# Where a one-core, four-layer kernel lays the zeros of its padded tensor, and which engine builds the first channels' taps

## The chip, the cores and the metric

The kernel runs on one core of a Trainium2 chip. The metric is device time in microseconds of one execution, as the median of several runs. The engines are named as in the profile: PE is TensorE's matmul and PEld its weight loads, DVE is VectorE, ACT is ScalarE, POOL is GpSimd and SP is SyncE, which here only issues DMA transfers. "Granted clock" is the share of full speed that TensorE was given.

## The reference

An image tensor `x` of 32 images, 192 channels and 56 x 56 pixels passes through four layers, each of the form `x = x + layer(groupnorm(x))`, with 32 groups of 6 channels. Cut to what matters:

```python
# layer 0: agent attention (6 heads, 49 agents) with a 3x3 depthwise convolution of v, then a projection
# layer 1: a two-way WKV scan over the 3136 pixels, sigmoid gate, layer norm, projection
# layer 2: each four channels are shifted by a rounded offset and smoothed with their own 3x3 Gaussian
x = x + _L0_conv_ref(_gn(x), ...)
x = x + _L1_conv_ref(_gn(x), ...)
x = x + _L2_conv_ref(_gn(x), L2_conv_offset)
# layer 3: convolution with a 55x55 implicit filter by FFT
x = x + _L3_conv_ref(_gn(x), ...)

def _L2_conv_ref(inp, offset):
    R = jnp.round(offset)                       # one (x, y) shift for each 4 channels
    x_src = jnp.arange(Wn)[None, :] - Ri[:, 0:1]
    x_ok = (x_src >= 0) & (x_src < Wn)          # zero where the shifted pixel lies outside
    ...
    kern = jnp.exp(-sq / (2.0 * SIGMA ** 2)); kern = kern / kern.sum(axis=(1, 2), keepdims=True)
    return conv_general_dilated(out, kern, ..., feature_group_count=Cn)
```

## The kernel before

The kernel has four stages in one program, one after the other; all data are float32.

1. `make_filter` builds the spectra of layer 3's filter (to about 164 us).
2. `attention` does layer 0, image by image: 32 turns of one loop. Two image tiles alternate: at the start of a turn the next image is loaded (`ready.image`, L392 and L394), and at its end the finished image is stored to the DRAM tensor `x1` (L863, L865), behind its sums `st_a` and `st_c` (L860, L862).
3. `scan_pairs` does layer 1 on pairs of images. It begins with loads of its weights (L936, L941, L942) and of attention's sums (L1063, L1065), prepares weights on PE (L955, L961), and then streams `x1` (L1018). Its result goes to the DRAM tensor `x2`.
4. `channel_blocks` does layers 2 and 3 channel by channel, in groups of six, for all 32 images at once.

`x2` is laid out for stage 4: for each channel 2 x 57 rows of 16 x 112 numbers, of which 56 hold an image row and the other 56 are a gap that must be zero, so that a row read at a shifted address runs into zeros. Attention writes these zeros: a small SBUF tile `zeros` (L460 sets it) is the source, and each channel's gaps are one DMA from SP (L869, 399 KB in 1824 pieces of 224 bytes). There are 192 of them, six at the end of each of the 32 image turns, right behind that image's stores. A dependency of the kind "NoSync" keeps them behind the store on SP's queue: it fixes the order of issue and waits for nothing.

Inside an image turn, `seen` is called twice: once for `gq` (when the first of four column blocks has been weighed) and once for the next image's `gk` (late in the turn); a further call stands ahead of the loop. Each copies a 65-row result into `once` and sends it to the constant tile `gq_c` or `gk_c` with one DMA on SP (L566, 597 KB), where it is repeated eight times. In the loop's second half, `moments` reads the next image (L485 and on).

In stage 4, `prepare(c)` is called four channels ahead of use. It loads a channel's shifted rows into one of three `shifted` tiles (L1618), multiplies them by the norm's scale on POOL (L1619), and applies the three horizontal taps: ACT makes the first (L1622) and, for each of the other two, a product in `more` (L1625), which POOL adds (L1626). `matrix(n)` builds, once for four channels, a 114 x 114 matrix that does the vertical shift and taps: three tap matrices (L1567), two additions (L1571, L1572), all on POOL, then one matmul (L1574) and a copy (L1576). `shift` loads the unshifted rows (L1635), multiplies by the matrix on PE (L1641) and adds (L1642); `middle` and `centre` take the group's mean off (L1661), and `analyse` and `synthesise` do the spectral convolution of the group before (L1683 to L1732). A tile with the tag `spare` has three buffers, which `more` and `sq` of `centre` share.

The order of instructions on each engine is not written out by hand: the framework orders them when the program is built, so that work that is ready earlier can stand ahead of its place in the text. Each engine then runs its own queue in that order.

The functions that the change touches, and what calls them, with the line numbers of the profile:

Of the kernel before, what the change touches and what calls it, by code (L numbers as in the profile page):

```python
# [23 lines left out]
ALU = mybir.AluOpType  # L24
# [4 lines left out]
C = 192  # L29
T = 96  # L30
S = 56
# [13 lines left out]
HA = HEADS * AG  # L45
GROUP = C // 32
# [361 lines left out]
def attention(ctx: ExitStack, tc: tile.TileContext, a, ready, x1, st_a, st_c, x2, gaps):  # L408
# [9 lines left out]
    nc = tc.nc  # L418
    NB = x1.shape[0]
# [9 lines left out]
    def psum():  # L429
        return pp.tile([128, 2, BANK], F32, name="ps", tag="ps")  # L430
# [4 lines left out]
    n = C + 1  # L435
# [9 lines left out]
    NK = len(WIDTHS)  # L445
# [12 lines left out]
    zeros = cp.tile([2 * (S + 1), LEAD], F32, name="zeros", tag="zeros")  # L458
    for t in (*agents_b[0], *agents_b[1], v_a, v_c, zeros):
        nc.gpsimd.memset(t, 0.0)  # L460
    for at in (0, x2.shape[0] - LEAD):
        nc.sync.dma_start(out=x2[at : at + LEAD].unsqueeze(0), in_=zeros[0:1])

    def small(name, shape):
        return sp.tile(shape, F32, name=name, tag=name)

# [88 lines left out]
    def seen(ag, w, to_c, name):  # L555

        ps = psum()
        for i, cols in enumerate((slice(0, 128), slice(128, C + 1))):
            n = (128, 65)[i]
            mm(ps[:n, i, : 4 * AG], w[0][:, cols], ag[0], start=True, stop=True)  # L560
            mm(ps[:n, i, 4 * AG : HA], w[1][:, cols], ag[1], start=True, stop=True)
        g = small(name, [128, HA])
        nc.scalar.copy(g, ps[:, 0, :HA])
        c = sp.tile([65, HA], F32, name="once", tag="once", bufs=1)
        nc.scalar.copy(c, ps[0:65, 1, :HA])
        nc.sync.dma_start(out=to_c[0:65], in_=c.unsqueeze(1).to_broadcast([65, 2 * NK, HA]))  # L566
        return g

    def normed(x, rs, nb, j):
# [72 lines left out]
    def turn_v(j, v):  # L642

        _, _, ns = sizes(j)
        vT = wp.tile([SUB, 4, 3 * 128], F32, name="vT", tag="vT")
        for s0 in range(0, ns, 2):
            ps = psum()
            for i in range(2):
                px = slice((s0 + i) * SUB, (s0 + i + 1) * SUB)
                for c in range(3):  # L650
                    nc.tensor.transpose(ps[:SUB, i, c * 128 : (c + 1) * 128], v[:, c, px], ident)
            nc.scalar.copy(vT[:, s0 : s0 + 2], ps[:SUB, :, : 3 * 128])
        return vT
# [152 lines left out]
    for b in range(NB):  # L806
        x, more = nxt, b + 1 < NB
        if more:
            nxt = ready.image(nc, a, b + 1)
        low, sums = small("low", [PAIR, NK, 3]), small("sums", [PAIR, NK, 3])  # L810
        got = sp.tile([PAIR, NK, C], F32, name="got", tag="got", bufs=1)
        turned, asked, back = {}, {}, {}
        for j in range(NK):
            prs = weigh(j, gk, low, sums)
            if j == 0:
                gq = seen(ag, wqT, gq_c, "gq_a")
            vT = turn_v(j, v[j])
            if j > 0:
                halves = gather(j - 1, *turned[j - 1])
            if j + 2 < NK:  # L820
                v[j + 2] = find_v(j + 2)
            turned[j] = turn(j, prs), vT
            if j > 0:
                settle(j - 1, halves, got)
            if j + 1 < NK:
                o[j + 1] = convolve(j + 1)
            elif more:
                mv, pools = moments(nxt)
        halves = gather(NK - 1, *turned[NK - 1])
        asked[0] = ask(0, gq)  # L830
        settle(NK - 1, halves, got)
        values = join(low, sums, got)
        done, o = o, {}
        st = small("st", [128, 2, 9])
        for t in range(1, NK + 2):
            if t < NK:
                asked[t] = ask(t, gq)
            if more and t == 1:
                mean, d = spread_of(mv)
            if more and t == 2:  # L840
                rs, nb = scaling(mean, d, pools)
                normed(nxt, rs, nb, 0)
            if t <= NK:
                back[t - 1] = turn_back(t - 1, asked[t - 1])
            if more and t in (3, 4):
                v[t - 3] = find_v(t - 3)
            if t >= 2:
                project(t - 2, done[t - 2], x, st)
            if t <= NK:
                answer(t - 1, back[t - 1], values, done[t - 1])  # L850
            if more and t == 2:
                ag = find_agents(b + 1, pools)
                normed(nxt, rs, nb, 1)
            if more and t == 3:
                gk = seen(ag, wkT, gk_c, "gk_a")
                normed(nxt, rs, nb, 2)
            if more and t == 4:
                o[0] = convolve(0)
                normed(nxt, rs, nb, 3)
        nc.sync.dma_start(out=st_a[:, b % 2, b // 2], in_=st[:, 0])  # L860
        for h, r in HALVES:
            nc.sync.dma_start(out=st_c[b % 2, :, h, b // 2], in_=st[r, 1])  # L862
        nc.sync.dma_start(out=x1[b, 0:128], in_=x[0].rearrange("p y x -> p (y x)"))  # L863
        for h, r in HALVES:
            stored = nc.sync.dma_start(  # L865
                out=x1[b, 128:C, 1568 * h : 1568 * h + 1568], in_=x[1][r].rearrange("p y x -> p (y x)")
            )
        for c in range(C * b // NB, C * (b + 1) // NB):
            laid = nc.sync.dma_start(  # L869
                out=gaps[c].rearrange("s h g w -> (s h) g w"),  # L870
                in_=zeros[:, 0:S].unsqueeze(1).to_broadcast([2 * (S + 1), NB // 2, S]),
            )
            behind = mybir.DependencyInfo(mybir.DependencyClass.NoSync, mybir.DependencyReason.DATA)
            tc.add_manual_dep(laid.ins, stored.ins.name, behind, reason="no burst")


class _Pairs:
# [640 lines left out]
def channel_blocks(ctx: ExitStack, tc: tile.TileContext, shifts, k, flat_x2, x2, rs2, spectra, out):  # L1518
# [8 lines left out]
    nc = tc.nc  # L1527
    NB = out.shape[0]
# [15 lines left out]
    for rows, shape in CHANNEL:  # L1544
        n = int(np.prod(shape))
        t = fixed[:rows, at : at + n]
# [15 lines left out]
    def matrix(n):  # L1562

        if n not in made:
            t = [wp.tile([PR, PR], F32, name=f"tap{f}", tag=f"tap{f}", bufs=1) for f in range(3)]
            for f in range(3):
                nc.gpsimd.tensor_scalar(  # L1567
                    t[f], diff_y, found[:, n, 6 + f : 7 + f], found[:, n, 3 + f : 4 + f], ALU.is_equal, ALU.mult
                )
            mat = wp.tile([PR, PR], F32, name="mat", tag="mat", bufs=3)  # L1570
            nc.gpsimd.tensor_tensor(t[0], t[0], t[1], ALU.add)  # L1571
            nc.gpsimd.tensor_tensor(mat, t[0], t[2], ALU.add)  # L1572
            ps = psum()
            nc.tensor.matmul(ps[:PR, :PR], lags, mat, start=True, stop=True)  # L1574
            rows = wp.tile([PR, PR], F32, name="rows", tag="rows", bufs=3)
            nc.vector.tensor_copy(rows, ps[:PR, :PR])  # L1576
            made.clear()
            made[n] = rows
        return made[n]

    def psum():
        return pp.tile([128, BANK], F32, name="ps", tag="ps", bufs=4)
# [16 lines left out]
    def prepare(c):  # L1599

        if c >= C:
            return
        n, j = divmod(c, GROUP)
        if j == 0:
            scales[n] = sp.tile([PR, GROUP, NI], F32, name="scale", tag="scale", bufs=3)
            for s in range(2):
                nc.sync.dma_start(
                    out=scales[n][(S + 1) * s : (S + 1) * (s + 1)],
                    in_=rs2[c : c + GROUP, s].partition_broadcast(S + 1),
                )  # L1610
        i = c // 4
        if c % 4 == 0:
            begin_at[i] = nc.values_load(
                begins[0:1, i : i + 1], engines=(mybir.EngineType.SP,), min_val=LEAD - S, max_val=LEAD + S
            )
        t = shifted[c % len(shifted)]
        there = flat_x2[bass.ds(begin_at[i] + c * SPAN, SPAN)].rearrange("(p g w) -> p g w", p=PR, w=PITCH)
        nc.sync.dma_start(out=t[:, :, 1 : S + 1], in_=there[:, :, 0:S])  # L1618
        nc.gpsimd.tensor_tensor(t, t, _bc(scales[n][:, j], [PR, NI, S + 2]), ALU.mult)  # L1619
        y = wp.tile([PR, NI, S], F32, name="smooth", tag="smooth", bufs=5)  # L1620
        taps = [found[:, i, f : f + 1] for f in range(3)]
        nc.scalar.activation(y, t[:, :, 0:S], AF.Copy, scale=taps[0])  # L1622
        for f in (1, 2):
            more = wp.tile([PR, NI, S], F32, name="more", tag="spare", bufs=3)
            nc.scalar.activation(more, t[:, :, f : f + S], AF.Copy, scale=taps[f])  # L1625
            nc.gpsimd.tensor_tensor(y, y, more, ALU.add)  # L1626
        smooth[c] = y
        rows_of[c] = matrix(i)
# [301 lines left out]
```

## Time and profile before

| What | Value |
|---|---|
| Median of 3 runs | 12221.74 us |
| Lowest, highest | 12216.5, 12241.55 us |
| The profiled execution's own time | 12216.98 us |
| Its span, first to last instruction | 12215.1 us |
| Mean granted clock of TensorE | 0.958 |
| Busy: PE, PEld, DVE, ACT, POOL | 90%, 54%, 88%, 59%, 28% |
| Instructions: DVE, ACT, POOL | 14722, 14690, 2568 |
| First and last zero transfer (L869) issued | 354.2 us, 4952.6 us |
| Stores of the last image issued | 4922.7 to 4928.2 us |
| First POOL instruction of the channel stage | 8444.3 us |

The span is cut by stage into about 0 to 164 us (filter), to 4923 us (attention), to 8444 us (scan) and to the end (channels). In rows of the timeline the first number is the start in us from the span's start, the second how long the row's instructions took from first to last, then the engine, the line, the operation, the tiles written and read, and how many. A name such as `SPq` or `DVEq` is an engine's queue. A bracket at the end of a row gives idle time ahead of it and what ended that. In rows of the waits, an engine and line are followed by what they waited for, the sum in us, how often, and the longest. Rows of the windows give the busy time of PE, PEld, DVE, ACT and POOL, with the number of instructions in brackets, then the granted clock, the mean share of time that the 16 DMA engines were busy, and what they moved.

### The profile page before, as it was taken

Reading aid. Unit: us, or ns where it says so; the run is one execution under the profiler, and the core shown is the slowest. Engines: PE = TensorE matmul, PEld = TensorE weight load, DVE = VectorE, ACT = ScalarE, POOL = GpSimd, SP = SyncE. Lnnn points to the kernel's source line nnn. Section 1 sums busy time; section 2 is a strip of 40 time slices with the busy share of each in tenths; the row PEclk is TensorE's granted clock in tenths of the full one; section 3 lists DMA queues with packets and bytes.
Section 4 is the critical chain, followed back from the end, with each engine's and each line's share of the span. In section 5 each row is a group of like instructions: output and inputs, shape, how many; then the busy total and the mean of one; then the engine's idle time right before and its main releaser. Section 6 shows DMA issues by size and latency. Waiting matters only on the chain. (4 is left out here: it accounts for less than half of the span.)

```text
span 12215.1 us, 157485 instructions
## 1 busy us (share of the span) xinstructions
PE 11030.6 (90%) x57358; PEld 6623.6 (54%) x57358; DVE 10753.1 (88%) x14722; ACT 7146.9 (59%) x14690; POOL 3400.5 (28%) x2568
## 2 busy tenths in 40 slices
PE   6999999999999999688888888886999999999999
PEld 3555555555555555333333333333666666666666
DVE  6888888888888888799999999996888899898897
ACT  3555555555555555466666666665666666666665
POOL 0000000000000000455555555555343343343330
PEclk9999999999999999899999999997999999999999
DMA  2222222222222222243334334334333333333331
GB/s 70 57 57 57 59 58 64 59 59 59 63 61 57 57 57 49 73 103 96 97 101 104 93 97 104 98 96 100 71 68 64 67 70 64 67 70 64 67 69 32
DMA packets 1959211, 876.56 MB, mean 72 GB/s; under 512 B 1821153, under 2 KB 1858292, under 8 KB 1949292
## 3 DMA queue, kind: packets, MB, share of 16 engines
q1 hardware_dynamic: 1948188, 840.69, 30.1%
q10 hardware_dynamic: 10240, 25.70, 0.8%
q8 instruction: 458, 7.50, 0.3%
q14 instruction: 325, 2.66, 0.1%
HBM read 482.13 MB, written 319.29 MB: 66 GB/s over the span
## 5 line engine op out<-in xcount | busy, mean ns | idle before, releaser
L619 DVE SCALAR_TENSOR_TENSOR o<-v_a,att_w,o 128x896 f32<-128x896 f32 (+1 forms) x1024 | 1056.8, 1032 | 467.3 <-ACT v_a L593 337.3
L1142 POOL MEMSET f<- 128x1 f32 x96 | 8.9, 99 | 4769.6 <-DMA st_c<-st 4764.6
L1793 ACT COPY y<-ps 64x252 f32<-64x252 f32 (+1 forms) x2376 | 808.7, 340 | 797.3 <-PE ps L1787 767.6
L1626 POOL TENSOR_TENSOR smooth<-smooth,more 114x896 f32<-114x896 f32 x384 | 866.3, 2259 | 1200.7 <-ACT more L1625 1141.2
L1709 PE MATMUL ps<-fixed,real 84*84 84x112 f32 x6144 | 1093.6, 260 | 0.0
L1709 PE MATMUL ps<-fixed,imag 84*84 84x112 f32 x6144 | 1091.1, 259 | 0.0
L1717 ACT ACTIVATE z<-ps,rs 84x112 f32<-84x112 f32 x3072 | 816.7, 355 | 322.1 <-PE ps L1709 319.5
L1709 PEld LDWEIGHTS ps<-fixed,real 84*84 84x84 f32 x6144 | 790.2, 154 | 158.4 <-issue 129.4
L1135 ACT ACTIVATE q<-q 128x784 f32<-128x784 f32 x384 | 328.5, 855 | 812.4 <-DVE q L1130 641.2
L1709 PEld LDWEIGHTS ps<-fixed,imag 84*84 84x84 f32 x6144 | 765.8, 153 | 0.0
L890 PE MATMUL ps<-sq,fixed 128*128 128x392 f32 x512 | 298.9, 746 | 425.9 <-ACT sq L1213 425.9
L636 ACT ACTIVATE pr<-ps,low 98x896 f32<-98x896 f32 (+1 forms) x384 | 352.3, 918 | 559.9 <-DVE low L634 559.9
L724 PE MATMUL ps<-gq_a,xs_a 128*112 128x294 f32 x1792 | 619.1, 427 | 45.7 <-DVE pq L729 45.7
L1787 PE MATMUL ps<-fixed,padded 114*128 114x168 f32 x3072 | 527.6, 322 | 134.6 <-DVE x L1729 118.3
L619 DVE SCALAR_TENSOR_TENSOR o<-v_c,att_w,o 128x448 f32<-128x448 f32 (+1 forms) x1024 | 638.3, 623 | 6.0 <-ACT v_c L604 0.9
L632 PE MATMUL ps<-xs_a,gk_a 128*98 128x448 f32 (+1 forms) x1536 | 637.1, 495 | 0.0
L633 PE MATMUL ps<-xs_c,gk_c 125*98 125x448 f32 (+1 forms) x1536 | 631.6, 492 | 0.0
L1728 PE MATMUL ps<-z,fixed 84*114 84x448 f32 x1536 | 609.7, 539 | 0.4 <-ACT z L1717 0.4
L725 PE MATMUL ps<-gq_c,xs_c 125*112 125x294 f32 x1792 | 608.3, 421 | 0.0
L890 PE MATMUL ps<-x,weights 128*128 128x392 f32 x1536 | 574.0, 517 | 31.1 <-DVE bv L1164 14.2
L737 ACT ACTIVATE pq<-pq 112x1176 f32<-112x1176 f32 x224 | 265.4, 1185 | 553.0 <-DVE pq L729 430.1
L1787 PEld LDWEIGHTS ps<-fixed,padded 114*128 114x128 f32 x3072 | 473.6, 198 | 206.1 <-DVE x L1729 140.5
(372 smaller groups left out, 29249.8 us busy)
## 6 DMA issues: line engine op xcount, KB each, us to landing
x<-x SPq DMA_DIRECT2D x576, 392.0 KB
x<-x SPq DMA_DIRECT2D x512, 196.0 KB
x<-zeros SPq DMA_DIRECT2D x192, 399.0 KB
shifted<-x SPq DMA_DIRECT2D x192, 399.0 KB
x<-x SPq DMA_DIRECT2D x192, 399.0 KB
out_x<-x SPq DMA_DIRECT2D x384, 196.0 KB
x<-in_x SPq DMA_DIRECT2D x32, 1568.0 KB
x<-x SPq DMA_DIRECT2D x32, 1568.0 KB
```

Of the source, the lines that this page charges most:

```text
L619: nc.vector.scalar_tensor_tensor(dst, tap(i), dww[:, t, i : i + 1], dst, ALU.mult, ALU.add)
L632: mm(ps[P2, h, :n], g[:, cols], xs_a[j][:, px], start=True, stop=False)
L633: mm(ps[P2, h, :n], gk_c[0:KC, 2 * j + h, cols], xs_c[j][0:KC, px], start=False, stop=True)
L724: mm(ps[:SUB, i, :HA], xs_a[j][:, px], g, start=True, stop=False)
L725: mm(ps[:SUB, i, :HA], xs_c[j][0:KC, px], gq_c[0:KC, 2 * j + (q + i) // ns], start=False, stop=True)
L890: mm(out, aa, srcs[t][h], start=True, stop=False)
L1626: nc.gpsimd.tensor_tensor(y, y, more, ALU.add)
L1709: nc.tensor.matmul(ps[:84, i * 2 * S : (i + 1) * 2 * S], part[:, i0 + i].rearrange("p s u -> p (s u)"), f3[:, m, :], start=(m == 0), stop= ...
L1717: nc.scalar.activation(z[:, i0 + i].rearrange("p m w -> p (m w)"), ps[:84, i * 2 * S : (i + 1) * 2 * S], AF.Copy, scale=q.rs[:, i0 + i : i ...
L1728: nc.tensor.matmul(got, f4[:, m, :], z[:, i0 : i0 + n, m, :], start=(m == 0), stop=(m == 1))
L1787: nc.tensor.matmul(ps[:, g * 168 : (g + 1) * 168], flat[:, (g0 + g) * 128 : (g0 + g + 1) * 128], f1, start=True, stop=True)
L1793: nc.scalar.copy(y[64 * m : 64 * m + 64, 2 * g0 + i : 2 * (g0 + n) : 2], got[64 * i : 64 * i + 64, :, :, m, :])
```

## The change

The 192 zero transfers are taken off one list, `bare`, in order. A new helper `lay(behind, n)` issues the next `n` of them, each kept behind the instruction `behind` on SP's queue in the same way as before (`issue_after` adds edges of issue order only). Two are laid behind each transfer of `gq_c` or `gk_c`, and four behind the last store of each image but the last, which lays whatever is left. When the list is empty, `lay` issues nothing.

In the channel stage, `matrix(n)` uses DVE for its five elementwise operations where `n` is 0 or 1 (channels 0 to 7), and POOL for all others as before. For channels 0, 2 and 4 the second and third tap are each one SCALAR_TENSOR_TENSOR on DVE (multiply by the tap, add to `y`) in place of ACT's product and POOL's addition. Channels 1, 3 and 5, and all from 6 on, stay as they were.

```diff
+    bare = list(range(C))
+
+    def lay(behind, n):
+
+        with tc.issue_after(behind.ins):
+            for c in bare[:n]:
+                nc.sync.dma_start(
+                    out=gaps[c].rearrange("s h g w -> (s h) g w"),
+                    in_=zeros[:, 0:S].unsqueeze(1).to_broadcast([2 * (S + 1), NB // 2, S]),
+                )
+        del bare[:n]
...
-        nc.sync.dma_start(out=to_c[0:65], in_=c.unsqueeze(1).to_broadcast([65, 2 * NK, HA]))
+        lay(nc.sync.dma_start(out=to_c[0:65], in_=c.unsqueeze(1).to_broadcast([65, 2 * NK, HA])), 2)
         return g
...
-        for c in range(C * b // NB, C * (b + 1) // NB):
-            laid = nc.sync.dma_start(
-                out=gaps[c].rearrange("s h g w -> (s h) g w"),
-                in_=zeros[:, 0:S].unsqueeze(1).to_broadcast([2 * (S + 1), NB // 2, S]),
-            )
-            behind = mybir.DependencyInfo(mybir.DependencyClass.NoSync, mybir.DependencyReason.DATA)
-            tc.add_manual_dep(laid.ins, stored.ins.name, behind, reason="no burst")
+        lay(stored, 4 if more else len(bare))
...
         if n not in made:
+            engine = nc.vector if n < 2 else nc.gpsimd
             t = [wp.tile([PR, PR], F32, name=f"tap{f}", tag=f"tap{f}", bufs=1) for f in range(3)]
             for f in range(3):
-                nc.gpsimd.tensor_scalar(
+                engine.tensor_scalar(
                     t[f], diff_y, found[:, n, 6 + f : 7 + f], found[:, n, 3 + f : 4 + f], ALU.is_equal, ALU.mult
                 )
...
-            nc.gpsimd.tensor_tensor(t[0], t[0], t[1], ALU.add)
-            nc.gpsimd.tensor_tensor(mat, t[0], t[2], ALU.add)
+            engine.tensor_tensor(t[0], t[0], t[1], ALU.add)
+            engine.tensor_tensor(mat, t[0], t[2], ALU.add)
...
         for f in (1, 2):
+            if c < GROUP and c % 2 == 0:
+                nc.vector.scalar_tensor_tensor(y, t[:, :, f : f + S], taps[f], y, ALU.mult, ALU.add)
+                continue
             more = wp.tile([PR, NI, S], F32, name="more", tag="spare", bufs=3)
```

## The prediction

> **What bounds the kernel now.** I read the page's slices first: PE is busy 90% of the span and DVE 88%, each near full for most of it, so the change can only matter where both stand still. Two such places show: a dent near slice 16 (attention gives way to the scan) and the start of the channel stage near 8445 us. I then read the windows, SP's queue and the waits at both, and one image of attention to see whether the zeros cost anything where they now lie.
>
> Stage border, columns: busy time of PE, PEld, DVE, ACT, POOL, then granted clock, DMA share, GB/s:
> ```profile
> 4930.00:4940.00 10.00, 0.00 (x0) 0.00 (x0) 0.00 (x0) 0.00 (x0) 0.00 (x0) 0.50 0.56 103
> 4940.00:4950.00 10.00, 0.00 (x0) 0.00 (x0) 0.00 (x0) 0.00 (x0) 0.00 (x0) 0.50 0.49 71
> 4950.00:4960.00 10.00, 0.00 (x0) 0.00 (x0) 0.00 (x0) 0.00 (x0) 0.00 (x0) 0.50 0.51 71
> ```
> No engine works for 30 us while the DMA engines move 71 GB/s. SP's queue over the same time (start, duration, what it issued), and PE's wait:
> ```profile
> 4926.92 1.23 SPq L865 DMA_DIRECT2D x<-x  x2
> 4928.19 30.03 SPq L869 DMA_DIRECT2D x<-zeros  x6
> 4958.33 5.58 SPq L936 DMA_DIRECT2D passing<-in_scan_o  x1
> ...
> 4965.85 1.83 SPq L1065 DMA_DIRECT2D seen<-st_c  x2
> ```
> ```profile
> PE ps L955 <- DMA x<-zeros: 44.3, 1, 44.3
> ```
> The last image's six zero transfers stand between its stores and the scan's first loads. PE waits 44.3 us in one piece.
>
> One image in the middle of attention, SP again:
> ```profile
> 2257.94 0.90 SPq L566 DMA_DIRECT2D gk_c<-once  x1
> 2274.72 0.33 SPq L863 DMA_DIRECT2D x<-x  x1
> ...
> 2279.95 30.77 SPq L869 DMA_DIRECT2D x<-zeros  x6
> 2310.76 5.77 SPq L392 DMA_DIRECT2D x<-in_x  x1
> 2316.58 1.18 SPq L394 DMA_DIRECT2D x<-in_x  x2
> 2317.87 0.94 SPq L566 DMA_DIRECT2D gq_c<-once  x1
> ```
> Here the same zeros hide: no engine's wait in 2280 to 2427 names a DMA, and PE idles under 10 us of that period. They are close to showing, though: the next image is first read by DVE (L485) at 2329.8, and the transfers end at about 2330.
>
> Start of the channel stage, POOL; the bracket is idle time and its releaser:
> ```profile
> 8469.65 4.23 POOL L1626 TENSOR_TENSOR smooth<-smooth,more 114x896 f32<-114x896 f32 x2
> 8505.77 4.22 POOL L1626 TENSOR_TENSOR smooth<-smooth,more 114x896 f32<-114x896 f32 x2 [2.09 <-ACT more L1625]
> 8515.77 0.43 POOL L1572 TENSOR_TENSOR mat<-tap,tap 114x114 f32<-114x114 f32 x1 [5.78 <-PE ps L1574]
> ```
> and DMA there:
> ```profile
> 8500.00:8510.00 10.00, 3.33 (x4) 1.09 (x4) 2.33 (x3) 2.91 (x3) 7.83 (x4) 0.67 0.42 89
> 8510.00:8520.00 10.00, 6.21 (x18) 4.11 (x18) 4.83 (x7) 0.00 (x0) 4.12 (x5) 0.50 0.18 37
> 8520.00:8530.00 10.00, 1.77 (x6) 1.34 (x6) 5.87 (x6) 5.63 (x6) 9.92 (x5) 0.50 0.21 46
> ```
> From 8450 to 8510 POOL is busy 53.6 of 60 us (sum of the six windows), DVE about 12. The chain of waits runs over POOL's L1567, L1619 and L1626 up to 8583, and over PE and DVE after it. The channel rows load at 0.46 DMA share and about 103 GB/s until 8508, then the DMA engines half idle for 18 us because SP waits (15.2 us at L1618) for a `shifted` buffer that the late POOL has not let go.
>
> **Part 1, zeros taken from the border.** The list of 192 channels shrinks by 2 ahead of the image loop and by 8 in each image (2 behind `gq_c`, 2 behind `gk_c`, 4 behind the stores). 2 + 23 x 8 = 186, so the 24th image lays the last 6, and images 25 to 32 lay none. At the border SP comes to L936 at about 4928.2 instead of 4958.3 (30.1 us), and without back-pressure its 5.58 us become about 0.4 like its neighbours, so the x loads of L1018 start at about 4932.2 instead of 4967.7: 35.5 us. In bytes: 6 x 399 KB = 2.45 MB at 71 GB/s is 34.5 us of queue. Against that: the last stores (2.35 MB at the 202 GB/s of 4920 to 4930) need 11.6 us from 4922.7, to 4934.3. If the scan's loads must wait until those land (a tile laid over theirs), they begin some 2 us later, at 4936, where their data began to flow at about 4966 before: 29, or 28 with one more such step. Nothing else is late next: all five engines are idle, and the scan runs on from there with DVE at 93%. Between 28 and 35.5 I take 33, nearer the byte count, since PE's L955 started within 1 us of the zeros' end. The granted clock is 0.50 there in either case, as PE still idles over 10 us.
>
> **Part 1, zeros inside attention.** Two zeros behind `gk_c`: 0.98 + 5.96 us of SP ((30.77 - 0.98) / 5 = 5.96 each), so SP is free at 2266 and the transfers (11.5 us, behind 3 to 5 for `gk_c`) end at 2273 to 2275; the next issue is at 2274.7. This hole covers them; were it gone, the stores would slip 1 to 2 us, for which only the image load waits, behind four more zeros. Four behind the stores are 0.98 + 3 x 5.96 = 18.9 us instead of 30.8, so the image and then `gq_c` are issued 11.9 us sooner: more slack. Two behind `gq_c`: SP's next issue is 80 us away. Cost 0. As a bound: images take 147.5 or 149.1 us (12 of 30 the long sort), with PE's clock at 0.97 in 2340 to 2400; another mix of these gives between -19 and +29, of which I allow -16 to +12, since attention starts in the same phase.
>
> **Part 2, taps and matrices.** Off POOL come two matrices (3 x 0.75 + 2 x 0.43 = 3.1 us each) and six L1626 (2.1 each): 6.2 + 12.6 = 18.8 of its 53.6. Off ACT come six L1625 (1.04 each). DVE gets ten small operations and six SCALAR_TENSOR_TENSOR; the nearest row is L619 on 128x896, 1.15 us, so 6.9 us into a DVE that is 80% idle there. For an even channel, 4.2 us of POOL become 2.3 us of DVE.
> How much reaches the path: the sixth channel's POOL work now ends at 8510. Loads set a floor: its x leaves SP at 8494.3 and lands near 8497, so at most about 14. POOL walked through (first `shifted` at 8458 as now; 1.74 a channel; 4.2 for each odd one; matrices 2 to 4 in the gaps; channel 5's `shifted` not before 8489, then 1.7 of POOL, one tap of ACT and 4.2) ends at 8497 to 8498: 12 less. What follows (mean, centring, channels 6 on, whose ACT tiles wait for POOL) hangs on that point, and the 18 us hole in the loads lets it move forward.
> Against it stands a row: L1661, a DVE operation with two SBUF inputs, takes 1.07 us at its least and 2.63 beside POOL; POOL's L1619 goes from 1.74 to 2.59, a tap from 0.75 to 3.42. If each of the six new ones met one POOL operation it would wait up to 2.1, and POOL would lose about 1 at each: near 6 less gain. In the worst case, a DVE wait in each chain and POOL still held by taps, the gain is -2. From -2 to 14 I take 11, nearer the walk, as DVE's pairs fall mostly into POOL's waits for loads.
> The Trainium skill (SBUF — State Buffer, Who interferes with whom) says that a DVE instruction with two SBUF inputs and a GpSimd one that reads SBUF exclude each other for a whole instruction; L1661's 2.63 us fits. By that rule alone every one of the six would block once and this part would bring 5; the sum would be 38.
>
> **Sum.** 33 + 0 + 11 = 44 us off the profiled execution's own 12216.98 (span 12215.1): 12173. The median of the three runs, 12221.74, lies 4.8 above that execution; I add 2: 12175. A measurement of this kernel tells 0.2%, or 24 us, from no change.
>
> **Rivals.**
> *Border only, 12186.* POOL keeps its present order: between channel 0's and channel 1's `shifted` it did 8.1 us of matrices 2 to 4, and if the DVE pairs also meet the locks, part 2 gives 0: 12219 - 33. For it: the order on POOL is not the program's, and L1661's spread. Against: 18.8 us leave the busiest engine. Chance 0.12.
> *Start only, 12208.* The zeros hid another wait at the border (stores landing, a tile laid over an older one) or SP issues the zeros late after all: `issue_after` fixes only what they stand behind. 12219 - 11. Against: stores end by 4934 by their bytes, and zeros are ready at once. Chance 0.08.
> *Slower, 12247.* SP takes `gq_c` and its two zeros ahead of the next image's load. Then six zeros precede the load as now, plus `gq_c`'s 3 us, and L485, which now reads within 1 us of landing, starts 3 us late in 24 images: +72, net 12175 + 72. It decides from 44 / 24 = 1.8 us an image. For it: `once` is ready at 2284.7, before SP is free. Against: today it was ready just as early and SP still took the image first. Chance 0.10, all slower outcomes included.
>
> **How the numbers follow.** Forecast 0.70, border only 0.12, start only 0.08, slower 0.10. Both first cases are over 24 us faster: faster 0.82; start only is within: 0.08; slower 0.10. Range: low 12219 - 35.5 - 14 - 16 = 12153; high 12219 - 28 + 2 + 12 = 12205, which leaves out the slower case and parts of the tails. The first two cases alone span 12153 to 12195.
>
> **What would show it.** Right: no zeros after about three quarters of attention; PE's wait at L955 falls from 44.3 to 8 to 16 us; image periods stay at 147.5 and 149.1; channel 5's last L1626 ends 10 to 14 us sooner after the stage's start than its 59.6 now; the 18 us hole in the loads shrinks. Wrong: a wait of PE or DVE for a DMA inside an image; L936 issued later than 4940; DVE's new operations at over 2 us; a channel period over the 114 to 115 us per six channels that the chain shows.

## The result: 0.6% slower, and the profile after

The changed kernel took 12308.13 us (median of 6 runs, 12298.35 to 12315.04) against 12227.83 us of the kernel before beside it (6 runs, 12216.5 to 12241.55): a ratio of 1.0064, interval 1.0051 to 1.0077. The forecast was 12175 us with a range of 12153 to 12205, so the time moved the wrong way and lies outside the range.

Cut at the same three places, the profiled executions show where the time went (us; attention to the last `st_a` store, then border and scan to the stage's first POOL instruction, then the channel stage to the end of the span):

| | attention | border and scan | channel stage | span |
|---|---|---|---|---|
| before | 4923.9 | 3520.5 | 3770.8 | 12215.1 |
| after | 5068.0 | 3490.4 | 3749.0 | 12307.5 |
| difference | +144.2 | -30.0 | -21.7 | +92.4 |

Border and start gained, as forecast, though the last column also holds differences of later groups that do not come from the change (see e3). Attention, which was to cost nothing, lost 144 us. (The change moved the lines: L485 is now L497, L619 is L631, the zeros of L869 are L470, L566 is L578, L872 and L874 are the stores of the sums, L936 is L942, L1567 to L1626 are L1574 to L1636.)

**Attention.** The waits of the whole kernel, DVE, hold one row that the kernel before has not at all:
```profile
DVE st_a L497 <- DMA x<-in_x: 167.8, 23, 8.6
```
DVE waits for the next image's load in 23 images, 7.3 us each. One of them, SP's queue first:
```profile
812.96 0.32 SPq L872 DMA_DIRECT2D st_a<-st  x1
...
817.34 18.68 SPq L470 DMA_DIRECT2D x<-zeros  x4
836.07 5.93 SPq L392 DMA_DIRECT2D x<-in_x  x1
...
843.50 0.93 SPq L578 DMA_DIRECT2D gq_c<-once  x1
844.49 15.21 SPq L470 DMA_DIRECT2D x<-zeros  x2
```
and DVE at that time:
```profile
842.65 0.68 DVE L631 SCALAR_TENSOR_TENSOR o<-v_c,att_w,o 128x448 f32<-128x448 f32 x1
850.58 1.68 DVE L497 BATCH_NORM_STATS2 st_a<-x 128x6 f32<-128x448 f32 x3 [7.25 <-DMA x<-in_x]
852.17 1.13 DVE L631 SCALAR_TENSOR_TENSOR o<-v_a,att_w,o 128x896 f32<-128x896 f32 x1
```
SP behaves as forecast: four zeros, the load, then `gq_c`. What the forecast did not have is the second view. Three of the seven statistics L497 stand between two rows of the convolution L631, where DVE arrives at 843.3, that is 30.4 us after the `st_a` store of that turn. In the kernel before DVE came to the first statistic 54.3 us after that store and did all seven there, as the image that the prediction shows has it:
```profile
2275.57 0.32 SPq L860 DMA_DIRECT2D st_a<-st  x1
...
2329.85 1.16 DVE L485 BATCH_NORM_STATS2 st_a<-x 128x6 f32<-128x448 f32 x2
```
The load is now issued 23.1 us after the store instead of 35.3, and DVE can read it at 850.6, 37.6 us after the store: 12 us of gain for the load, but 7.3 us too late for a read that was moved ahead by 24. PE's and ACT's orders in attention are those of before in the traces; on DVE only these three statistics and one small addition of `got` have changed places in each image.

The other engines, in windows of 10 us (busy PE, PEld, DVE, ACT, POOL, granted clock, DMA share, GB/s), and PE's wait for the weights that ACT makes from DVE's result:
```profile
840.00:850.00 10.00, 9.98 (x100) 7.52 (x99) 3.32 (x5) 8.47 (x20) 0.00 (x0) 1.00 0.90 240
850.00:860.00 10.00, 7.49 (x24) 3.25 (x22) 9.42 (x13) 0.00 (x0) 0.00 (x0) 0.99 0.66 124
860.00:870.00 10.00, 5.88 (x56) 5.24 (x57) 10.00 (x17) 4.70 (x9) 0.00 (x0) 0.50 0.33 47
```
```profile
PE ps L663 <- ACT pr L648: 143.2, 23, 6.2
```
DVE is busy 3.3 of 10 us, PE then stands 6.2 us, once in each of the 23 images, and the granted clock is 0.50 in that window. The first 23 image periods are 154.8 us on average, against 148.2 before: 23 x 6.6 = 151 us lost. The seven later ones, which have no zeros ahead of their loads, take 146.7 to 146.8, less than any image before (10 us back), and the last is 3 us longer: 144 in all.

**Border.** PE's wait, then SP:
```profile
PE ps L961 <- DMA passing<-in_scan_o: 10.5, 1, 10.5
```
```profile
5071.07 1.23 SPq L877 DMA_DIRECT2D x<-x  x2
5072.62 0.98 SPq L942 DMA_DIRECT2D passing<-in_scan_o  x1
```
The 44.3 us for the zeros are gone, 10.5 us for the scan's first weights remain. From attention's last DVE operation to the scan's first reduction it is 20.7 us, before 54.6: 33.9 less. Border and scan together are 30.0 shorter; in the other kernels without zeros at the border they are 28 to 35 shorter (3485 to 3492 us), so the scan itself varies by some us.

**Start of the channel stage**, POOL (the stage begins at 8558.47) and two of DVE's new operations:
```profile
8566.65 2.35 POOL L1574 TENSOR_SCALAR tap<-fixed,found 114x114 f32<-114x114 f32 x3 [6.75 <-DVE tap L1578]
...
8606.44 2.59 POOL L1626 TENSOR_TENSOR shifted<-shifted,scale 114x928 f32<-114x928 f32 x1 [1.27 <-DMA shifted<-x]
8611.12 4.23 POOL L1636 TENSOR_TENSOR smooth<-smooth,more 114x896 f32<-114x896 f32 x2 [2.09 <-ACT more L1635]
```
```profile
8585.19 1.20 DVE L1632 SCALAR_TENSOR_TENSOR smooth<-shifted,found,smooth 114x896 f32<-114x896 f32 x1 [5.51 <-ACT smooth L1629]
8586.85 2.42 DVE L1632 SCALAR_TENSOR_TENSOR smooth<-shifted,found,smooth 114x896 f32<-114x896 f32 x1
```
Channel five's last addition ends 56.9 us after the stage's start, before 65.6: 8.7 less. Of the six new DVE operations four take 1.15 to 1.21 us and two 2.42 and 2.10. Each of the six ran beside a POOL operation, and each time one of the two took longer: DVE's those two, and for the other four POOL's, a tap of 1.65 us (0.76 otherwise), an L1636 of 2.80 (2.08) and L1626 of 2.25 and 2.59 (1.74). In e11, below, the last two of the six met no POOL operation, and both took 1.15.

### The profile page after: what moved, and what is told of

It reads as the page before. It is cut to its first block, busy times and chain, and to the rows that moved or that the text cites. A ratio compares the mean times of both kernels' runs of the same rounds, so it can differ in the third digit from the quotient of the medians.

```text
span 12307.5 us, 157444 instructions
## 1 busy us (share of the span) xinstructions
PE 11075.2 (90%) x57358; PEld 6667.9 (54%) x57358; DVE 10760.2 (87%) x14738; ACT 7140.3 (58%) x14684; POOL 3317.1 (27%) x2552
## 5 line engine op out<-in xcount | busy, mean ns | idle before, releaser
L631 DVE SCALAR_TENSOR_TENSOR o<-v_a,att_w,o 128x896 f32<-128x896 f32 (+1 forms) x1024 | 1052.7, 1028 | 422.4 <-ACT v_a L605 292.5
L1636 POOL TENSOR_TENSOR smooth<-smooth,more 114x896 f32<-114x896 f32 x378 | 851.8, 2257 | 1175.1 <-ACT more L1635 1119.6
L631 DVE SCALAR_TENSOR_TENSOR o<-v_c,att_w,o 128x448 f32<-128x448 f32 (+1 forms) x1024 | 633.8, 619 | 3.1 <-ACT v_c L616 0.9
```

The source lines that it names most:

```text
L631: nc.vector.scalar_tensor_tensor(dst, tap(i), dww[:, t, i : i + 1], dst, ALU.mult, ALU.add)
```

## The experiments

Theory A, formed from these views: the zeros and taps do what was forecast, and the loss is three statistics that the build moved ahead of the load's landing. Rivals: the zeros cost by themselves where they now lie (DMA traffic beside the engines, or the queue behind `gq_c`), or the taps cost. To hold an instruction behind another is to add an edge of issue order, as `lay` does. The kernel before ran beside each of three sets of runs: 12225.7 us (27 runs) beside the first four, 12223.2 (9) beside the next four, 12225.84 (7) beside the last three.

**e1: all of `moments` held back.**
```diff
-                mv, pools = moments(nxt)
+                with tc.issue_after(lows[1].ins):   # the second pooled maximum of this column block
+                    mv, pools = moments(nxt)
```


> The changed kernel with one thing added: the statistics of the next image (L485's BATCH_NORM_STATS2 and all that follows in moments) are kept behind the second maximum of the last column block on DVE's queue, which is where they stood before the change. Zeros and taps stay as changed. Theory A (the loss is DVE's order: three statistics moved ahead, DVE stands 7.3 us in 23 images for a load that has not landed): those waits vanish, image periods 146.7 to 147.5, time 12307 - 23 x 7 = about 12140 to 12160. Theory B (the zeros behind gq_c and gk_c themselves take the time, by crowding the image load or the engines): periods stay near 154, time 12295 to 12315.

Measured: 12205.19 us, ratio 0.9981 (0.9972 to 0.999). DVE waits for no load in attention, as A says, and attention is 105 us shorter than in the changed kernel. The other 39 of the 144 us stay: the images take 149.5 us on average, 1.3 more than before, and the total missed A's number, 12140 to 12160, by 45 us. This hold had moved a memset and the sort's maxima on DVE as well; e5 repeats it with less moved.

**e2: the taps alone** (the kernel before with part 2 of the change).

> The kernel before with only the second part of the change: taps of channels 0, 2, 4 and matrices 0 and 1 on DVE. Theory A: channel 5's last addition on POOL ends 8.8 us sooner after the stage's start, and the stage as a whole is 9 to 22 us shorter, so 9 to 22 us faster than before. Theory C (the DVE operations block POOL, or reorder the channel stage, and cost time): as slow as before or slower, by up to 60.

Measured: 12206.93 us, ratio 0.9983 (0.9974 to 0.9992). Images of 147.5 and 149.1 and 44.3 us at the border as before; the first group's `rs` on ACT comes 92.4 us after the stage's start, before 101.1. Part 2 is worth about 19 us (10 to 32 by the interval) and costs nothing, as A says.

**e3: the zeros alone** (the changed kernel with the taps of before).

> The changed kernel with taps and matrices back on POOL and ACT, so only the zeros are moved. Theory A: attention as in the changed kernel (23 periods of about 154.4, then 146.8), border 34 us shorter than before, channel stage as before: 9 to 22 us slower than the changed kernel, 12316 to 12331. Theory C: faster than the changed kernel.

Measured: 12314.84 us, ratio 1.0077 (1.0063 to 1.0091); the wait for the load is there in full:
```profile
DVE st_a L497 <- DMA x<-in_x: 166.9, 23, 8.9
```
The loss is part 1's and has nothing to do with the taps. The total is just under the 12316 to 12331 expected. By the medians this kernel is 6.7 us slower than the changed one (two sets of runs), where e2 gave 19, so part 2 is worth some 7 to 19 us. The profiles leave it as open: the channel stage takes 3742 to 3768 us in the eleven kernels with part 2, on average 3753, and 3764 and 3771 in the two without.

**e4: seven zeros behind the stores, none elsewhere.** In this build DVE keeps the order of before, but for the last turn with zeros: only three are left for it, and there the three statistics are moved ahead.
```diff
-        lay(nc.sync.dma_start(out=to_c[0:65], ...), 2)
+        nc.sync.dma_start(out=to_c[0:65], ...)
...
-        lay(stored, 4 if more else len(bare))
+        lay(stored, 7 if more else len(bare))
```


> The changed kernel with seven zero transfers behind each image's stores and none behind gq_c or gk_c; the list runs out in the 28th image, so the border is free too. DVE's order is that of before (the built program shows it), but the next image's load is issued 6 us later than before. Theory A in its wider form (what costs is the load's landing against DVE's first read of it, wherever the zeros lie): in the trace of before the load had at most a microsecond or two to spare, so DVE now waits 3 to 6 us at L485's place in 27 images, +80 to +160, less 34 at the border and 9 to 22 in the channel stage: 12250 to 12320. Theory B: nothing lies behind gq_c and gk_c, periods 147.5 as before: 12160 to 12180.

Measured: 12230.92 us, ratio 1.0005 (0.9996 to 1.0014).
```profile
DVE st_a L497 <- DMA x<-in_x: 36.0, 28, 3.0
```
With the old order and one zero more ahead of the load, DVE comes 54.4 us after the store and can read at 55.7 on average: a wait of 1.3 us an image. That is smaller than expected, and the total is below the 12250 to 12320 of A, but it is the same mechanism from the other side: at 6.0 us a zero ((55.7 - 37.7) / 3, with the mean of the changed kernel's four), the kernel before stood some 5 us from this wait, less than one zero transfer. Attention grew by 63 us and ate what border and start gave; 36 of them are these waits, the rest was not followed up.

**e5: the order of before, zeros and taps as changed.** Only the statistics and the two sums `by_x` are held; DVE's order in attention is then that of before.
```diff
+        with tc.issue_after(behind.ins) if behind is not None else ExitStack():
             for i in range(7):
                 nc.vector.bn_stats(st_a[:, i], ...)
...
-                mv, pools = moments(nxt)
+                mv, pools = moments(nxt, lows[1] if b > 0 else None)
```


> The changed kernel, with only the next image's normalisation statistics and its two column sums (eleven bn_stats, two bn_aggr, two by_x sums) held behind the second pooled maximum of the same column block, so that DVE, PE and ACT go through attention in the order of the kernel before; the zeros and the taps stay as changed. In the first held kernel other rows had moved too (a memset and the maxima of the sort), and its images took about 149.6 us instead of 148.2. Theory A (the reordered statistics wait for the load, and that alone is the loss): no wait of DVE for the image load, images of 147.5 or 149.1 as before, so that the 1.4 us an image of the first held kernel come back, and the sum of the prediction holds: the kernel before less 34 for the border and less 9 to 19 for the start, 12172 to 12183. Theory B (zeros between gq_c, gk_c and the stores cost something by themselves, DMA traffic beside the engines): periods stay at 150 or above, and the time above 12230 less the border's 34, about 12190 to 12210 as in the first held kernel.

Measured: 12162.08 us, ratio 0.9953 (0.9939 to 0.9966). Images of 147.5 and 149.1, no wait for the load, the last `st_a` store at 4924.97, before 4923.86. The same zeros at the same places on SP cost nothing to speak of once DVE's order is the old one, so theory B falls. This is the kernel that the prediction described, and it lies within the prediction's range, 13 us below its number and 10 below what was expected of this run.

**e6: six zeros behind `gq_c`, none elsewhere; DVE's order as changed.**
```diff
-        lay(nc.sync.dma_start(out=to_c[0:65], ...), 2)
+        lay(nc.sync.dma_start(out=to_c[0:65], ...), 6 if name == "gq_a" else 0)
...
-        lay(stored, 4 if more else len(bare))
+        lay(stored, 0 if more else len(bare))
```


> The changed kernel with six zeros behind gq_c and none behind gk_c and the stores, so that the next image's load stands directly behind the stores; DVE keeps the reordered statistics of the change, the first three of the seven ahead by a third of a column block. Theory A (landing of the load against the first read): the load is issued 19 us sooner than in the changed kernel and lands before DVE comes to it, so DVE waits for no DMA, and all 31 periods are those of the images without zeros, 146.7 us: attention about 45 us shorter than before, total 12128 to 12140. Theory B (the reordered statistics cost by themselves, or the zeros anywhere in an image cost): periods of 154 or above in the first 23 images or more, total above 12300.

Measured: 12126.28 us, ratio 0.9922 (0.9908 to 0.9935), the fastest of all that ran and 2 us under what was expected. SP and DVE in one image:
```profile
933.81 0.32 SPq L872 DMA_DIRECT2D st_a<-st  x1
...
940.47 0.34 SPq L392 DMA_DIRECT2D x<-in_x  x1
...
944.09 0.92 SPq L578 DMA_DIRECT2D gq_c<-once  x1
945.06 37.55 SPq L470 DMA_DIRECT2D x<-zeros  x6
```
```profile
964.10 1.67 DVE L497 BATCH_NORM_STATS2 st_a<-x 128x6 f32<-128x448 f32 x3
965.69 1.14 DVE L631 SCALAR_TENSOR_TENSOR o<-v_a,att_w,o 128x896 f32<-128x896 f32 x1
```
The three statistics stand where they stand in the changed kernel, 30.3 us after the store, with no bracket: the load is there. Images take 146.8 us on average, and attention is 43.8 us shorter than before. So the moved order is not bad in itself; it is better, if its data has come.

**e7: four zeros behind `gk_c`, four behind the stores.**
```diff
+        lay(nc.sync.dma_start(out=to_c[0:65], ...), 4 if name == "gk_a" else 0)
```


> The changed kernel with four zeros behind gk_c and four behind the stores, none behind gq_c; DVE's order as changed. Theory A (four zeros behind the stores put the load's landing about 7 us behind the reordered read): the same wait of 6 to 8 us in some 24 images, periods of about 154, total 12295 to 12320. Theory B (the two zeros behind gq_c share the DMA engines with the load issued just ahead of them and so delay it): the wait falls away or to under 2 us, periods of 146.7 to 148, total 12130 to 12180.

Measured: 12520.2 us, ratio 1.0244 (1.023 to 1.0258), slower than either theory said.
```profile
825.89 19.71 SPq L470 DMA_DIRECT2D x<-zeros  x4
845.70 5.71 SPq L875 DMA_DIRECT2D x<-x  x1
851.51 0.38 SPq L872 DMA_DIRECT2D st_a<-st  x1
```
```profile
889.92 1.68 DVE L497 BATCH_NORM_STATS2 st_a<-x 128x6 f32<-128x448 f32 x3 [16.98 <-DMA x<-in_x]
```
The load lands 38.4 us after the `st_a` store, as in the changed kernel (37.6), but the store itself comes late: four zeros behind `gk_c` do not fit into the hole of 17 us between its issue and the first store (2257.94 to 2274.72 in the kernel before), SP passes the first store at 851.4, and DVE, which does not wait for stores, is by then 9 us further on. The wait becomes 16.8 us an image, and the first 23 periods 164.1. Two zeros fit there (e5), four do not. That zeros behind `gq_c` delay the load is out: with none there it lands at the same 38 us.

**e8: e6's zeros, e5's order.**

> As the second kernel of this set (six zeros behind gq_c, none elsewhere), but with the statistics held as in the first kernel of this set, so that DVE's order in attention is that of the kernel before. It tells whether the moved statistics are worth something by themselves once the load is there in time. If the order is worth 1.4 us an image: periods of 147.5 and 149.1 as before, total 12172 to 12183. If it is the early load that makes short periods: 146.7 in all images, total 12128 to 12140.

Measured: 12174.25 us, ratio 0.9958 (0.9945 to 0.9972), images of 147.5 and 149.1. As expected of the case that the order is what counts: the load that came sooner is worth nothing by itself; the moved order is worth 48 us (12174.25 - 12126.28). Where it comes from is the page's row of the convolution, whose last part is DVE's idle time ahead of it; the first is e8, the second e6:
```profile
L633 DVE SCALAR_TENSOR_TENSOR o<-v_a,att_w,o 128x896 f32<-128x896 f32 (+1 forms) x1024 | 1055.0, 1030 | 469.8 <-ACT v_a L607 340.1
```
```profile
L631 DVE SCALAR_TENSOR_TENSOR o<-v_a,att_w,o 128x896 f32<-128x896 f32 (+1 forms) x1024 | 1054.6, 1030 | 418.4 <-ACT v_a L605 291.5
```
In the old order, here of e8, DVE idles about 1.5 us in an image for ACT's next `v_a`; in e6 three statistics of 1.67 us in all fill that place.
```profile
2315.65 1.15 DVE L633 SCALAR_TENSOR_TENSOR o<-v_a,att_w,o 128x896 f32<-128x896 f32 x1 [1.49 <-ACT v_a L607]
```
Over the kernel that is 340.1 - 291.5 = 48.6 us. The rows of the other kernels agree: 332.8 to 340.1 in all six with the old order or the statistics held, 291.5 to 295.4 in all that moved them.

**e9 and e10: three and two zeros behind the stores** (and four and five behind `gq_c`), DVE's order as in e6: a test of the rule that the wait is the load's landing less DVE's arrival.

> The kernel with all zeros behind gq_c, but with four there and three behind the stores; DVE's order as in that kernel (three statistics moved ahead). Theory A as a rule of two times: DVE wants the image 30.4 us after the st_a store of the same turn; the image landed 37.6 us after it with four zeros ahead and 56.1 with seven, that is 6.2 us a zero, so 31.4 with three. Expected: a wait of about 1 us (0.4 to 2) in each of some 27 images, periods of 147.7 to 148.5, and a total of 12150 to 12180. Theory B (the wait is not this difference, but comes with zeros behind the stores at all): a wait of 5 us or more in each, periods of 152 or above, total above 12250.

> As the kernel before in this set, with five zeros behind gq_c and two behind the stores. By the rule of two times the image lands 25.2 us after the st_a store, 5 us ahead of DVE's read at 30.4: no wait of DVE for the load, periods of 146.7, total as with all zeros behind gq_c, 12118 to 12135. Theory B: a wait of 3 us or more in each image, total above 12190.

Measured: e9 12151.12 us, ratio 0.9939 (0.9922 to 0.9955); e10 12131.78 us, ratio 0.9922 (0.9905 to 0.9938), with no wait for the load. e9:
```profile
DVE st_a L497 <- DMA x<-in_x: 26.5, 27, 1.9
```
That is 1.0 us in each of 27 images, as the rule gave. Its images average 147.4 us, a little under the 147.7 to 148.5 expected.

**e11: tap tiles of their own for DVE's two matrices**, in e6.
```diff
-            t = [wp.tile(..., tag=f"tap{f}", bufs=1) for f in range(3)]
+            t = [wp.tile(..., tag=f"tap{f}" if n > 1 else f"early{f}", bufs=1) for f in range(3)]
```


> The kernel with all zeros behind gq_c, with the first two matrices, which DVE builds, on three tap tiles of their own instead of the three that POOL's matrices use. In the changed kernel POOL's first tap started 8.2 us after the stage's first operation, behind DVE's last tap, against 6.0 before. If the shared tiles are what it waits for: POOL's first tap at about 6.0 to 6.5, channel five's last addition at 54.5 to 55.5 instead of 57.1 after the stage's start, and in the total at most 2 us, 12116 to 12132. If they are not: 8.2 and 57.1 again.

Measured: 12139.69 us, ratio 0.9932 (0.9916 to 0.9949); the time is above the expected 12116 to 12132, and the kernel is no faster than e6. POOL's first tap starts 6.0 us after the stage's start (8.5 in e6), so it did wait for the shared tiles. But channel five's last addition ends at 56.8, in e6 at 57.1:
```profile
8428.02 1.74 POOL L1626 TENSOR_TENSOR shifted<-shifted,scale 114x928 f32<-114x928 f32 x1 [4.05 <-DMA shifted<-x]
```
Almost all that POOL saves goes into a longer wait for channel five's rows (4.05 us; 1.73 in e6), which can be read 48.7 us after the stage's start in both. So the expected 54.5 to 55.5 did not come.

## Why the prediction was wrong, step by step

The kernels that decide it, one to a line: the load of the next image and DVE's first read of it, in us after the `st_a` store of the same turn. The load's first 128 channels, which the statistics `st_a` read, are 128 pieces of 12544 bytes; the end of the last of them is from the DMA records of the same traces.

| kernel | zeros ahead of the load | last piece ends at | DVE comes at | DVE reads at | wait each | image period |
|---|---|---|---|---|---|---|
| e4 | 7 | 54.3 | 54.4 | 55.7 | 1.3 | 150.8 mean |
| before | 6 | 48.0 | 54.3 | 54.3 | 0 | 147.5 or 149.1 |
| e5 | 4 | 36.1 | 54.3 | 54.3 | 0 | 147.5 or 149.1 |
| after | 4 | 36.4 | 30.4 | 37.7 | 7.3 | 154.8 mean |
| e9 | 3 | 30.0 | 30.4 | 31.4 | 1.0 | 147.4 mean |
| e10 | 2 | 24.6 | 30.3 | 30.3 | 0 | 146.8 mean |
| e6 | 0 | 15.0 | 30.3 | 30.3 | 0 | 146.8 mean |

(The ends are medians of the first 23 images, waits and reads with a wait are means. The mean periods are over the images with zeros ahead of the load; for e6, e9 and e10 over all 30 periods but the last.) A zero more ahead of the load puts its end 5.9 us later ((54.3 - 24.6) / 5), and where DVE waits, it reads 1.3 to 1.4 us after that end.

- **Zeros inside attention: the step that failed.** "the image and then `gq_c` are issued 11.9 us sooner: more slack ... Cost 0." The first half held: two zeros fewer let the load's last piece end 11.6 us sooner (48.0 and 36.4). "Cost 0" took DVE's read at 54.3 us for a fixed time. It is the build's choice, and three statistics were put 24 us sooner. The cost is 144 us: the 23 images with a wait of 7.3 us are each 8.0 us longer than the later ones, 184 us in all; the new order gives back 1.4 us in each of 30, 42 us; the last period is 3 us longer; the sum is within 1 us of the 144. The Trainium skill (TensorE: Matmul & The Clock Gate, the section on the array's 16 sub-arrays) says that VectorE works its queue strictly in order; the 7.25 us in which DVE starts none of the L631 rows queued behind the statistics, though ACT's `v_a` for the next of them was there at 844.8, agree with it.
- **Its own warning** was the right one: "a wait of PE or DVE for a DMA inside an image", at the very L485 that it named as close to showing. That it named this place was in part luck. What ends at 2330 in the image shown is the transfer of `gq_c` (pieces of 1176 bytes); the pieces that L485 reads end at 2323.6, 6.3 us before the read, not "within 1 us". The warning was listed as something to look for afterwards and given no price for the case that the reader moves, not the load.
- **The rival "Slower"** had the place (DVE's first read against the landing) and the threshold of 1.8 us an image, but not the mechanism: SP took the image ahead of `gq_c`, as the prediction argued. Its 3 us would also not have been enough, with some 5 to spare by the table (48.0 and 1.3 against 54.3). At 0.10 it stood for all slower outcomes.
- **Border: right.** 33 forecast, 33.9 measured up to the scan's first work and 30.0 over border and scan; PE's wait 10.5, in the forecast 8 to 16.
- **Start: right, a little over.** 11 forecast, 8.7 measured at channel five. The sign "10 to 14 us sooner ... than its 59.6 now" has a slip: 59.6 counts from POOL's first tap (8450.3), not from the stage's start, from where it is 65.6. Counted from the first tap it is now 48.7, 10.9 less, but that tap itself comes 2.2 us later. The hole in the loads did shrink: no window of 10 us between 8610 and 8650 has a DMA share under 0.36, where it was 0.18 and 0.21. The floor was off: "channel 5's `shifted` not before 8489" is 44.7 us after the stage's start, it came at 48.0 in the changed kernel, held by its load. e11 shows that the shared tap tiles are not the reason. The operations that the prediction feared would block each other did so in all six cases, but each time only one of the two lost, 0.5 to 1.3 us, where the prediction priced 2.1 for DVE and 1 for POOL; its sign "DVE's new operations at over 2 us" came in two of them. How much of that reached the path was not tested. In the timed runs the part is worth 7 to 19 us (e3, e2); what may lie beyond the 8.7 could not be given to any instruction, since the later groups of six differ by several us between kernels of equal order there, and stays open.
- **Sum.** With DVE's order of before it holds: 12175 forecast, 12162 measured (e5). With the order that the build chose and the load in time: border 34, taps 19 and 44 of attention from 12223 give 12126, and 12126.28 was measured (e6). That this agrees to the microsecond is luck: the 19 has an interval of 10 to 32, and e6's own profile splits its gain into 43.8, 33.2 and 14.1.

Open: why the build moved the statistics. In the kernels here where nothing holds them they were moved where up to four zeros stand between the stores and the load, and stayed where six or seven did; e4 has both in one program. This fits a plan that lets a reader move once its load is issued sooner. That is argued from the built orders, not tested.

## What to carry to other kernels

When a change moves a DMA and the order of instructions is made at build time, compare the built order of every engine that reads its data, not only the queue that was moved: a transfer that lands sooner can still be late for a reader that was put ahead of it. Give each such pair two times measured from one event, landing and arrival; their difference is the wait, and it returns in every turn of the loop. What it adds to a turn can be more or less than the wait: 8.0 us for 7.3 here, 17.3 for 16.8 in e7, 0.6 for 1.0 in e9. A reader moved ahead into another wait of its engine is a gain (here 1.5 us an image), so first move the load, by putting the filler behind it, and only then judge the new order.

## What the runs showed that was not expected

- A gap of about 1.5 us on DVE, repeated in 31 images, was worth more than the whole border's 34: filling it took 48 us off (e6 against e8).
- The kernel before was near an edge that its waits do not show: one 399 KB zero transfer more ahead of the load (about 6 us at 224 bytes a piece) turned no wait into 1.3 us in each of 28 images (e4).
- Four zeros behind `gk_c` in place of two behind each of `gk_c` and `gq_c` cost 212 us (12520.2 - 12308.13, runs of two sets), since SP then issues the stores, and with them the load behind, 9 us late in 23 images.
